# Four heads at a time in the maxima of two blocks, a third pair of PSUM banks, and a new order: a transformer kernel on one core

## The chip, the cores and the metric

The kernel runs on one core of a Trainium2 chip. The metric is the time of one execution on the device, in microseconds (us). The core has five engines, which run their own instruction streams and wait for each other by semaphores: TensorE (PE; PEld is its weight load), VectorE (DVE), ScalarE (ACT), GpSimd (POOL) and SyncE (SP), which here only issues DMAs. Matrix products are written to PSUM, which has eight banks of 128 partitions x 512 numbers of four bytes; VectorE and ScalarE read them from there.

## The reference

Two layers over an input of 4 sequences of 512 tokens with 128 features. Only the first attention is touched by the change; the rest sets the surroundings.

```python
def _L0_attn_ref(x, WQ, WK, WV, WO):                      # 16 heads of 8 features
    Q, K, V = (heads(WQ), heads(WK), heads(WV))
    score = einsum('bhqd,bhkd->bhqk', Q, K) / sqrt(8) + mask      # causal
    score = exp(score - max(score, axis=-1, keepdims=True))
    score = score / sum(score, axis=-1, keepdims=True)
    out = einsum('bhqk,bhkd->bhqd', score, V)
    return out.transpose(0, 2, 1, 3).reshape(B, S, E) @ WO
...
x = x + _L0_attn_ref(_layernorm(x), ...)
x = x + _L0_ffn_ref(_layernorm(x), ...)    # 8 experts, top 2, capacity, gelu, 128 -> 512 -> 128
x = x + _L1_attn_ref(_layernorm(x), ...)   # a gated linear recurrence over time, then a gelu layer
x = x + _L1_ffn_ref(_layernorm(x), ...)    # five ternary matrices, silu and gelu
```

## The kernel before

**Blocks and stages.** The work is cut into four blocks, one for each sequence (`NB` = 4, 512 tokens each, `TB` = 4 tiles of 128). Each block runs through eight stages: `project` (queries, keys, values), `maxima` (the largest score of each row), `weights` (exponentials and the product with the values), `output` (projection, then `route`: which two experts a token goes to, and a scatter of its row to DRAM), `experts` (gather, 8 experts with 176 seats each, gather back), `recurrence` (8 chunks of 128 channels: four products with the tile `rw`, a scan on VectorE), `feed` and `ternary`. The last block's `feed` and `ternary` are done in two halves.

**Who puts the instructions in order.** The stages only record tasks (`Plan.note`). `Plan.order` then walks through time with costs for each operation (`cost`), and takes for the engine that can begin first the task with the largest weight: the longest chain of costs behind it, plus an offset from the table `AHEAD`, one number for each stage and block. What it decides is each engine's fixed order of instructions. It also keeps a model of TensorE's clock and, where TensorE would wait for more than 0.4 us by its costs, puts products of the constant tile `spread` with itself into a free bank (`fillers`; their line is L513). Their results are never read. All recorded instructions are issued by one line, L524, so the profile's groups go by the names of the tiles.

**PSUM.** Pool `p_d` has three single banks (tag `pt`), which nearly every stage uses. Pool `p_s` has two pairs of banks (tag `s`), for the attention: a task that needs a pair takes it from `pair()`. When the attention has ended, the pairs are given to `p_d` as four more banks (`take`). One bank (`po`) collects the product with the values. `Slots` hands the banks out; the planner gives a task that which has been free longest.

**The scores.** Four groups of four heads; a head lies on 32 partitions, so that four products with 32 rows can run side by side in TensorE's array. `maxima` makes for each group and each part of the rows (tile 3; tile 2; tiles 1 and 0) the scores against all keys up to the diagonal, adds the mask by a product with an identity matrix (tile `mask_q`), and reduces with a maximum on VectorE into `mx`. Block 0 does one head at a time in a single bank, so a group has 12 such tasks; the other blocks two heads in a pair. The maxima are split into two rounded parts (`mh`), transposed (`mT`, in block 0 under the tag `hl`), and in `weights` a product with `spread` subtracts them in PSUM. `weights` then works on four heads, with both pairs at once: product, subtraction, one exponential for each pair on ScalarE into `ex`, masking of the diagonal on GpSimd or VectorE, product with the values into `po`.

In the profile's names: `mx<-pt` and `mx<-s` are the reductions, `s<-ks,qs` or `pt<-ks,qs` as an output of TensorE the scores of one of the two stages, `ex<-s` the exponentials, `hT` the experts' Gelu, `xgd<-ya` the scatter, `xg<-xgd` the experts' load, `st<-dec,k` the scans, `r_h_w` and `r_w_w` the ternary weights. ScalarE holds one table of functions at a time; Exp and Gelu are in different ones, and a change is an instruction of its own (ACT_TABLE_LOAD).

Of the kernel before, what the change touches and what calls it, by code (L numbers as in the profile page):

```python
# [20 lines left out]
P = 128  # L21
# [22 lines left out]
def block_kernel(ctx: ExitStack, tc: tile.TileContext, i: dict, out: bass.AP):  # L44
# [9 lines left out]
    class Slots:  # L54


        def __init__(self, pool, tag, count):
            self.pool, self.tag, self.count = pool, tag, count
            self.size, self.dtypes = 0, set()
            self.until = [0.0] * count  # L60
            self.free = list(range(count))
            self.queues = {}

        def lay(self):
            dtype = F32R if F32R in self.dtypes else min(self.dtypes, key=str)
# [1 line left out]
                self.pool.pool.tile([P, self.size], dtype, name=f"{self.tag}_{k}") for k in range(self.count)  # L67
            ]

        def take(self, other):  # L70

            n = other.size // self.size
            self.taken = other, n
            for k in range(other.count):
                for _ in range(n):
                    self.free.append(len(self.until))
                    self.until.append(other.until[k])
            other.free = []

        def lay_taken(self):  # L80
            other, n = self.taken
            for t in other.tiles:
                self.tiles += [t[:, x * self.size : (x + 1) * self.size] for x in range(n)]

    class Lent:


        def __init__(self, slots, shape, dtype):
            self.slots, self.shape, self.dtype = slots, shape, dtype
            self.slot, self.left, self.end = None, 0, 0.0  # L90

        def dims(self, ap):
            if len(self.shape) == 2:
# [104 lines left out]
    class Plan:  # L198
# [142 lines left out]
        def begin(self, task, engine):  # L341

            t = self.now[engine]
            if task.table is not None and task.table != self.table:
                t += TABLE
            for e, r in task.ready.items():
                if e != engine and r > t:
                    t = r
            new = [x for x in task.lents if x.slot is None]
            for lent in new:  # L350
                same = [x for x in new if x.queue is lent.queue]
                free = lent.slots.free
                if len(free) < len(same) or any(x not in same for x in lent.queue[: len(same)]):
                    return None
                t = max(t, sorted(lent.slots.until[k] for k in free)[len(same) - 1])
            return t


# [28 lines left out]
        def order(self):  # L387
# [5 lines left out]
            for task in self.tasks:  # L393
                if task.stage and task.stage[-1].isdigit():
                    task.weight += AHEAD[task.stage[:-1]][int(task.stage[-1])]
            self.now = dict.fromkeys(ENGINES, 0.0)
            self.table, self.dma = None, 0.0
            self.window, self.active, self.warm = 0, 0.0, False
# [13 lines left out]
            while len(self.log) < len(self.tasks):  # L412
# [37 lines left out]
                items, took, after = task.ways[engine]  # L450
                for lent in task.lents:
                    if lent.slot is None:
                        s = lent.slots
                        lent.slot = min(s.free, key=lambda k: s.until[k])
                        s.free.remove(lent.slot)
                        lent.queue.remove(lent)
                if task.table is not None:
                    self.table = task.table
# [19 lines left out]
                for lent in task.lents:  # L478
                    lent.begun = True
                    lent.left -= 1  # L480
                    lent.end = max(lent.end, end)
                    if lent.left == 0:
                        lent.slots.until[lent.slot] = lent.end
                        lent.slots.free.append(lent.slot)
                task.engine = engine
                for e in task.ways:
                    can[e].remove(task)
# [16 lines left out]
        def issue(self):  # L504
            done = self.order()
            for s in self.slots.values():
                s.lay()
            self.slots["p_d", "pt"].lay_taken()
            self.recording = False
            last = None  # L510
            for task in done:
                if isinstance(task, Fill):
                    nc.tensor.matmul(  # L513
                        task.slots.tiles[task.k][:, : task.n], lhsT=spread[:, 0, :],
                        rhs=spread.rearrange("p g n -> p (g n)")[:, : task.n], start=True, stop=True,
                    )
                    continue

                if task.puts and last is not None and last.puts is task.puts:
                    tc.nc.gpsimd.memset(between, 0.0)  # L520
                if task.engine == "POOL":
                    last = task
                for op, args, kw in task.ways[task.engine][0]:
                    task.ins = getattr(getattr(nc, NAMES[task.engine]), op)(  # L524
                        *map(self.real, args), **{k: self.real(v) for k, v in kw.items()}
                    )
                for x in task.puts or ():
                    if x is not task and x.ins is not None:
                        tc.declare_no_dep(task.ins.ins, x.ins.ins, reason="a row of its own for each token and choice")


    AHEAD = {
        "experts": (1093, -30, 183, 214),
        "feed": (-513, -466, 303, -412),
        "maxima": (-14, 173, -113, 124),
        "output": (912, 246, -21, 373),
        "project": (255, -57, 11, -73),
        "recurrence": (69, 208, 89, -280),
        "ternary_0_": (-1, 4, -2, -244),
        "ternary_2_": (0, 0, 0, 147),  # L540
        "weights": (-86, 98, 268, 497),
    }
    TABLE, NEAR, PATIENCE = 1.3, 0.1, 4.0
    NAMES = {"DVE": "vector", "ACT": "scalar", "POOL": "gpsimd", "SP": "sync", "PE": "tensor"}
# [1 line left out]
    def cost(engine, op, out, ins, kw, args):  # L546
# [39 lines left out]
        if op == "tensor_copy":  # L586
            return 0.2 + 8.0e-4 * n, 0.1
        return 0.25 + 2.1e-3 * n if n > 64 else 1.2, 0.1

    plan = Plan()  # L590

# [186 lines left out]
    def maxima(b):  # L778

        mx = At.att.tile([P, TB, NG, NG], F32, tag="mx", name="mx")  # L780
        for g in range(NG):

            n = 1 if b == 0 else 2
            for part in ((3,), (2,), (1, 0)):
                for h in range(NG // n):
                    ps = bank("s1", shape=(P, 1, S)) if b == 0 else pair()
                    at = 0
                    for t in part:
                        product(ps, h, qs[:, g, ts(t, P)], ks[:, g, :], 0, (t + 1) * P, at, start=(at == 0), n=n)
                        at += (t + 1) * P  # L790

                    at, w = part[0] * P, len(part)
                    with one_task():
                        for j in range(n):
                            mm(ps[:, j, at : at + w * P], lhsT=identb, rhs=mask_q[:, : w * P],
                               start=False, stop=True, skip_group_check=True)
                    at = 0
                    for t in part:
                        nc.vector.tensor_reduce(
                            mx[:, t, g, ts(h, n)], ps[:, :, at : at + (t + 1) * P], AX.X, ALU.max, negate=True,  # L800
                        )
                        at += (t + 1) * P
            hi, lo = mh[:, :, :, 2 * g], mh[:, :, :, 2 * g + 1]
            nc.vector.tensor_copy(hi, mx[:, :, g, :])
            nc.vector.tensor_tensor(lo, mx[:, :, g, :], hi, ALU.subtract)
# [756 lines left out]
```

## Time and profile before

| | |
|---|---|
| median of 3 runs | 741.08 us (740.5 to 745.08) |
| the profiled execution | 740.8 us |
| its span, first to last instruction | 739.1 us |
| TensorE busy | 661.6 us (90%), 3698 products in the records |
| VectorE busy | 462.5 us (63%) |
| ScalarE busy | 307.0 us (42%) |
| GpSimd busy | 198.3 us (27%) |
| granted TensorE clock, mean | 0.943 of full speed |
| table loads on ScalarE | 30, 38.5 us |
| filling products (L513) | 95.2 us busy |

A line of a group reads: line, engine, operation, output<-input by the program's names, shapes, count | busy time in us, mean ns of one | idle time of the engine just before them, and what ended it. Busy times are unions of intervals, and matmuls are pipelined, so a busy TensorE is not one at its peak; a product in four-byte numbers is recorded as two. A line of the table of stretches gives for each engine the busy time and, in brackets, the number of instructions, then the granted clock of TensorE (PEclk, 1.00 is full speed), the share of the DMA engines and GB/s.

Where the stages of the first two blocks lie, by the first and last instruction of their tiles: block 0's reductions from 17.6 to 70.4 us, its exponentials from 34.3 to 85.6, its output projection from 91.2; block 1's reductions from 94.7 to 135.7, its exponentials from 141.4 to 202.2, its output projection from 209.8; block 0's experts' Gelu from 132.4 to 192.3. The scans of the four recurrences begin at 227.1, 337.0, 533.2 and 603.1.

### The profile page before, as it was taken

The page shows a single profiled execution, that of the slowest core. Times are in us where ns is not written, and L with a number is a line of the kernel's source. Part 1 is how long each engine was busy: PE and PEld are TensorE (multiplying, and loading weights), DVE is VectorE, ACT ScalarE, POOL GpSimd, SP SyncE. Part 2 cuts the span into 40 slices and gives each one's busy share as a digit, 9 for nine tenths or more (in the row PEclk, how much of TensorE's full clock was granted, in tenths as well). Part 3 has the DMA queues.
Part 4 walks back from the last instruction along what each step waited for, and adds up shares of the span by engine and source line. Part 5 has one row for each costly group of instructions (what it writes and reads, how often), then busy time and mean ns, then how long its engine had stood idle before and what let it go on. Part 6 is the DMA issues. An engine that isn't in the chain of part 4 may idle for free.

```text
span 739.1 us, 10411 instructions
## 1 busy us (share of the span) xinstructions
PE 661.6 (90%) x3698; PEld 407.4 (55%) x3698; DVE 462.5 (63%) x1125; ACT 307.0 (42%) x496; POOL 198.3 (27%) x295
## 2 busy tenths in 40 slices
PE   5999978978887999999999988979899989999795
PEld 2545454644562358553445644777775454557685
DVE  6875498372278775485889771356527776675444
ACT  2134500688631234566351466751552234322222
POOL 3122213183254000163023234127204030113121
PEclk9579995899998999999999999999999999999898
DMA  5630002252311315301200002352343102000000
GB/s 128 180 87 2 1 20 64 86 170 78 93 44 54 92 26 171 115 23 33 61 22 15 1 19 65 104 149 83 86 144 96 44 21 58 8 1 15 1 1 19
DMA packets 72364, 45.78 MB, mean 62 GB/s; under 512 B 9712, under 2 KB 65264, under 8 KB 72304
## 3 DMA queue, kind: packets, MB, share of 16 engines
q1 hardware_dynamic: 69680, 40.58, 19.4%
q0 software_dynamic: 2048, 4.20, 2.0%
q8 instruction: 31, 0.51, 0.3%
q10 hardware_dynamic: 576, 0.26, 0.1%
q14 instruction: 29, 0.24, 0.1%
HBM read 35.45 MB, written 9.57 MB: 61 GB/s over the span
## 4 chain that ended last, share of the span: by engine, by line
PE 40%; DVE 6%; ACT 5%; issue 2%; POOL 1%; DMA 1%; ACTq 0%; DVEq 0%; SPq 0%
PE s L524 18%; PE pt L524 17%; PE s L513 4%; ACT h L524 1%; DVE h L524 1%; PE po L524 1%; POOL xgd L524 1%; ACT L524 1%; DMA xg<-xgd 1%; ACT ex L524 1%; DVE mx L524 1%; DVE hh L524 1%; ACT hT L524 0%; DVE yc L524 0%; DVE f L524 0%
## 5 line engine op out<-in xcount | busy, mean ns | idle before, releaser
L524 PE MATMUL pt<-yTr,rw 128*128 128x512 f32 x192 | 95.8, 616 | 4.4 <-DVE taken L524 3.1
L524 ACT ACTIVATE ex<-s 128x768 f32<-128x768 f32 (+1 forms) x96 | 79.4, 879 | 43.3 <-PE s L524 40.5
L524 DVE TENSOR_REDUCE mx<-s 128x2 f32<-128x512 f32 (+3 forms) x96 | 74.7, 816 | 8.1 <-PE s L524 7.3
L524 POOL TENSOR_SCALAR_AFFINE_SELECT ex<-ex 128x256 f32<-128x256 f32 (+1 forms) x78 | 38.5, 496 | 128.6 <-ACT ex L524 122.5
L524 PEld LDWEIGHTS pt<-yTr,rw 128*128 128x128 f32 x192 | 34.6, 193 | 43.6 <-issue 23.6
L524 POOL DMA_INDIRECT xg<-ygd,rt_at x32 | 33.8, 1057 | 74.5 <-DMA ygd<-xg 66.0
L513 PE MATMUL s<-spread 128*128 128x128 f32 (+1 forms) x214 | 47.2, 360 | 7.4 <-DVE h L524 3.0
L524 POOL TENSOR_TENSOR ln_rs<-ln_rs,mhalf 128x4 f32<-128x4 f32 (+2 forms) x22 | 24.3, 1105 | 107.6 <-DVE ln_rs L524 107.4
L524 PE MATMUL po<-ex,vs 128*9 128x128 f32 (+3 forms) x512 | 50.4, 441 | 0.7 <-DVE ex L524 0.4
L513 PEld LDWEIGHTS s<-spread 128*128 128x128 f32 x214 | 37.4, 203 | 17.6 <-DVE h L524 3.7
L524 PE MATMUL pt<-xT,ew 128*128 128x176 f32 x200 | 41.5, 333 | 5.8 <-ACT hT L524 3.4
L524 ACT ACTIVATE hT<-pt,w_mb 128x176 f32<-128x176 f32 x100 | 34.5, 407 | 25.6 <-PE pt L524 25.0
L524 POOL DMA_INDIRECT xgd<-ya,rt_at x32 | 31.6, 986 | 48.1 <-DVE rt_incl L524 42.0
L524 POOL CAST hh<-h 128x512 fp32r<-128x512 f32 (+1 forms) x19 | 12.0, 638 | 113.2 <-ACT h L524 58.3
L524 ACT ACT_TABLE_LOAD x30 | 38.5, 1283 | 5.2 <-issue 3.1
L524 DVE TENSOR_TENSOR_SCAN st<-dec,k 128x512 f32<-128x512 f32 x32 | 39.3, 1232 | 1.0
L524 PEld LDWEIGHTS pt<-xT,ew 128*128 128x128 f32 x200 | 31.6, 196 | 13.2 <-ACT hT L524 6.8
L524 PE MATMUL s<-ks,qs 32*128 32x256 f32 (+3 forms) x192 | 34.4, 434 | 3.1 <-DVE mx L524 2.4
L524 DVE TENSOR_REDUCE mx<-pt 128x1 f32<-128x256 f32 (+3 forms) x64 | 27.6, 484 | 9.8 <-PE pt L524 9.5
L524 PE MATMUL s<-yTr,rw 128*128 128x512 f32 x64 | 32.0, 606 | 1.2 <-DVE k L524 0.7
L524 PE MATMUL pt<-hT,ew 128*128 128x176 f32 x160 | 30.1, 322 | 3.3 <-ACT hT L524 2.4
L524 PE MATMUL s<-qs,ks 32*128 32x512 f32 (+3 forms) x256 | 27.5, 391 | 3.4 <-ACT ex L524 2.1
(305 smaller groups left out, 1331.2 us busy)
## 6 DMA issues: line engine op xcount, KB each, us to landing
ew<-in_E_dram SPq DMA_DIRECT2D x64, 256.0 KB, 2.9
xg<-xgd SPq DMA_DIRECT2D x4, 704.0 KB, 5.0
ygd<-xg SPq DMA_DIRECT2D x12, 192.0 KB, 2.1
rw<-in_Wk_dram SPq DMA_DIRECT2D x32, 64.0 KB, 2.0
rw<-in_Wv_dram SPq DMA_DIRECT2D x32, 64.0 KB, 1.9
rw<-in_Wq_dram SPq DMA_DIRECT2D x32, 64.0 KB, 1.9
rw<-in_Wg_dram SPq DMA_DIRECT2D x32, 64.0 KB, 2.1
h<-in_h_w_dram SPq DMA_DIRECT2D x8, 256.0 KB, 3.0
```

What stands on the lines that cost most here:

```text
L513: nc.tensor.matmul(task.slots.tiles[task.k][:, : task.n], lhsT=spread[:, 0, :], rhs=spread.rearrange("p g n -> p (g n)")[:, : task.n], sta ...
L524: task.ins = getattr(getattr(nc, NAMES[task.engine]), op)(*map(self.real, args), **{k: self.real(v) for k, v in kw.items()})
```

## The change

Three things are done at once.

1. In blocks 0 and 1 (`FOURS`), `maxima` handles all four heads of a group in one task, in two pairs of banks, with one reduction for each pair and tile. Blocks 2 and 3 stay at two heads.
2. Two of the three single banks of `p_d` are laid out as one tile of 1024 columns (`joint`), so that they can be lent as a third pair to tasks of the stages in `WIDE` (maxima and softmax of blocks 0 and 1) while both are free. `open`, `get` and `put` of `Slots` do the bookkeeping, in the planner's time. Other tasks still use the two banks singly. In the profile the two banks then bear the name `joint` instead of `pt`.
3. The table `AHEAD` has new numbers, so the order of the instructions differs everywhere, in all blocks.

The instructions that do the work are otherwise the same; the line numbers move (L513 to L559, L524 to L570).

```diff
+        def lay_joint(self, lender):
+
+            self.lay()
+            lender.count -= 2
+            lender.lay()
+            lender.count += 2
+            (dtype,) = {t.dtype for t in lender.tiles}
+            both = lender.pool.pool.tile([P, 2 * lender.size], dtype, name="joint")
+            lender.tiles += [both[:, : lender.size], both[:, lender.size :]]
+            self.tiles.append(both)
+
+        def open(self, lent):
+
+            got = [(self.until[k], k) for k in self.free]
+            if self.lender is not None and lent.wide:
+                n = self.lender.count
+                if n - 1 in self.lender.free and n - 2 in self.lender.free:
+                    got.append((max(self.lender.until[n - 2 : n]), self.count))
+            return got
+
+        def get(self, lent, t):
+
+            k = min(self.open(lent), key=lambda x: (max(x[0], t), x[1]))[1]
...
     AHEAD = {
-        "experts": (1093, -30, 183, 214),
-        "feed": (-513, -466, 303, -412),
-        "maxima": (-14, 173, -113, 124),
-        "output": (912, 246, -21, 373),
-        "project": (255, -57, 11, -73),
-        "recurrence": (69, 208, 89, -280),
-        "ternary_0_": (-1, 4, -2, -244),
-        "ternary_2_": (0, 0, 0, 147),
-        "weights": (-86, 98, 268, 497),
+        "experts": (943, 252, 1024, -23),
+        "feed": (-778, 135, -10, -1375),
+        "maxima": (110, 118, -386, 62),
+        "output": (673, 292, 171, 695),
+        "project": (-292, -658, 682, -1001),
+        "recurrence": (260, -843, -240, -730),
+        "ternary_0_": (522, -135, -50, -154),
+        "ternary_2_": (0, 0, 0, 70),
+        "weights": (303, 416, 1206, 155),
     }
...
+    WIDE = {"maxima0", "weights0", "maxima1", "weights1"}
+    FOURS = {0, 1}
...
-            n = 1 if b == 0 else 2
+            n = NG if b in FOURS else 2
             for part in ((3,), (2,), (1, 0)):
                 for h in range(NG // n):
-                    ps = bank("s1", shape=(P, 1, S)) if b == 0 else pair()
+                    pss = [pair() for _ in range(n // 2)]
+                    ps = [p[:, j] for p in pss for j in range(2)]
                     at = 0
                     for t in part:
-                        product(ps, h, qs[:, g, ts(t, P)], ks[:, g, :], 0, (t + 1) * P, at, start=(at == 0), n=n)
+                        with one_task():
+                            for j in range(n):
+                                own = ts(n * h + j, HP)
+                                mm(ps[j][:, at : at + (t + 1) * P], lhsT=qs[own, g, ts(t, P)],
+                                   rhs=ks[own, g, 0 : (t + 1) * P], start=(at == 0), stop=False, skip_group_check=True)
                         at += (t + 1) * P
...
-                    at = 0
-                    for t in part:
-                        nc.vector.tensor_reduce(
-                            mx[:, t, g, ts(h, n)], ps[:, :, at : at + (t + 1) * P], AX.X, ALU.max, negate=True,
-                        )
-                        at += (t + 1) * P
+                    for k, p in enumerate(pss):
+                        at = 0
+                        for t in part:
+                            nc.vector.tensor_reduce(
+                                mx[:, t, g, ts(n // 2 * h + k, 2)], p[:, :, at : at + (t + 1) * P], AX.X, ALU.max,
+                                negate=True,
+                            )
+                            at += (t + 1) * P
```

## The prediction, made before the changed kernel was run

> **What bounds the kernel now.** I read the page's busy rows first, then a table of stretches cut where the stages of block 0 and block 1 begin and end, then the groups of the maxima's reductions and of ScalarE inside those stretches, and last the timeline of TensorE.
>
> The stretches are: maxima and softmax of block 0 (17.6 to 70.8), maxima of block 1 beside block 0's routing (91.2 to 137), experts of block 0 beside the softmax of block 1 (131 to 204), everything up to the last block's recurrence (204 to 599), and the end.
>
> ```profile
> core 0: us, PE busy (x) PEld busy (x) DVE busy (x) ACT busy (x) POOL busy (x), PEclk, DMA share, GB/s
> 17.60:70.80 53.20, 50.52 (x301) 26.26 (x299) 40.12 (x120) 15.64 (x21) 9.78 (x17) 0.74 0.34 98
> 91.20:137.00 45.80, 38.54 (x205) 25.46 (x206) 37.53 (x98) 7.18 (x12) 9.55 (x16) 0.70 0.11 34
> 131.00:204.00 73.00, 61.14 (x473) 39.62 (x472) 28.32 (x62) 53.49 (x77) 30.72 (x45) 0.96 0.37 109
> 204.00:599.00 395.00, 364.90 (x1994) 221.31 (x1994) 258.29 (x628) 175.27 (x295) 112.30 (x148) 0.98 0.24 67
> 599.00:739.10 140.10, 123.36 (x548) 84.33 (x547) 83.07 (x172) 41.10 (x75) 25.08 (x32) 0.96 0.06 16
> ```
>
> Four different limits stand in five rows. In the first, TensorE is busy 50.5 of 53.2 us, much of it at half clock (0.74 granted). In the second VectorE leads (37.5 of 45.8) and TensorE is throttled again. In the third ScalarE carries 53.5 of 73 us. From 204 on TensorE is busy 92% of the time, and it sets the pace.
>
> ```profile
> L524 DVE TENSOR_REDUCE mx<-pt 128x1 f32<-128x512 f32 x16 | 10.3, 686 | 2.8 <-PE pt L524 2.5
> L524 DVE TENSOR_REDUCE mx<-s 128x2 f32<-128x1024 f32 x8 | 9.5, 1219 | 2.5 <-PE s L524 2.5
> L524 DVE TENSOR_REDUCE mx<-pt 128x1 f32<-128x384 f32 x16 | 8.3, 552 | 4.8 <-PE pt L524 4.8
> L524 DVE TENSOR_REDUCE mx<-s 128x2 f32<-128x768 f32 x8 | 7.6, 954 | 0.8 <-PE s L524 0.6
> L524 DVE TENSOR_REDUCE mx<-pt 128x1 f32<-128x256 f32 x16 | 6.0, 417 | 2.2 <-PE pt L524 2.2
> L524 DVE TENSOR_REDUCE mx<-s 128x2 f32<-128x512 f32 x8 | 5.5, 691 | 2.4 <-PE s L524 2.1
> ```
>
> The first form of each size is block 0 (one head), the second block 1 (two heads). Reading two heads at once saves little: 1219 ns against 2 x 686.
>
> ```profile
> L524 ACT ACT_TABLE_LOAD x16 | 20.5, 1283 | 2.2 <-PE pt L524 1.4 <-issue 0.3 <-DVE xg L524 0.2
> L524 ACT ACTIVATE ex<-s 128x768 f32<-128x768 f32 (+1 forms) x24 | 19.9, 879 | 1.7 <-PE s L524 1.5
> L524 ACT ACTIVATE hT<-pt,w_mb 128x176 f32<-128x176 f32 x32 | 11.3, 403 | 10.2 <-PE pt L524 10.1
> ```
>
> These are ScalarE's groups between 131 and 204: switching between Exp and Gelu costs as much (20.5 us) as all 24 exponentials.
>
> **Block 0's maxima.** One head at a time becomes four. TensorE's part shrinks: 64 products of 32 rows took 19.7 us in the first stretch, partly cold; four such products side by side are what the softmax does already (28.9 us for four blocks, 7.2 each). So 12 us leave TensorE; the 48 mask products (9.5 us) stay. VectorE's reductions go from 28.4 us (16 x 0.686, 0.552, 0.417, 0.279) to 26.2 (8 x 1.219, 0.954, 0.691, 0.413).
>
> That stage now hangs on VectorE. A rule speaks against the change here: the Trainium skill, TensorEngine Tiling (Array Packing), Performance Considerations, says that packing speeds TensorE but not the emptying of PSUM, which may become the bottleneck. The rows agree. If TensorE set the pace, the stage would gain 12 us; by the rule it gains 28.4 - 26.2 = 2.2. I take the rule. A set of four heads needs both pairs of banks; in block 0 the lent pair lets the next set be filled while the second half of the last is reduced (TensorE needs some 1.0 us: 0.50 for the products, 0.28 for the first two masks, two hand-overs; a half takes 1.1 to 1.2).
>
> In the order of the changed program the whole of block 0's maxima stands ahead of its first softmax product; before, the two were interleaved. So I add them: 26.2 us of reductions, 1.5 for the four splits, 3.5 for the statistics of blocks 1 and 2 between them, from 17.6: 48.8. Then four groups of softmax at some 10.5 us, from the timeline (three units of products 0.6 to 1.0, two exponentials 1.94 or 1.51, hand-overs 0.4: 3.4 + 2.6 + 2.6; the flip of the output with copy and reciprocal 1.9): 42. The output stage follows at about 94; before, its projection started at 91.2. **Cost 3 us** (bounds: a gain of 5, if groups overlap more; a loss of 12, if each set is 1 us late).
>
> **Block 1's maxima.** The third pair is hardly lent here: in the built order all 24 reductions of block 1 read the two own pairs, and one single exponential of blocks 0 and 1 reads the lent one. A set holds both pairs, so nothing is filled while it is reduced. Per set 1.0 + 2.44, 0.95 + 1.9, 1.25 + 2.2, four times: 39 us, and 8 us of routing on VectorE between them: 47. Before, they took 44 (92.3 to 136.2). **Cost 3 us**, on the start of block 1's softmax. Waiting behind are its first exponentials; the experts of block 0 wait for routing and gather alone, and these keep their place.
>
> **Table loads.** Built, ScalarE has 38 loads before and 28 after; 8 of each belong to the path not taken, so 30 become 20. Of these, 16 become 10 between the start of block 0's experts and the end of block 1's softmax: 6 x 1.283 = 7.7 us less on the engine that carries this stretch. The page on ScalarE: Activation LUTs (What ACT_TABLE_LOAD costs) gives 2.66 us for each switch, with a drain; then it would be 16.0 us. The timeline shows no such drain:
>
> ```profile
> 140.06 1.28 ACT L524 ACT_TABLE_LOAD   x1
> 141.35 1.94 ACT L524 ACTIVATE ex<-s 128x1024 f32<-128x1024 f32 x2
> ```
>
> The next activation starts 1.29 us after the load. I take 7.7. Idle time of ScalarE there is 12 to 20 us, mostly on TensorE; the later start of the softmax (3 us) is hidden in part by the order, which puts 16 Gelus ahead of the first exponential where 8 stood. I count **a gain of 5 us** for the stretch. The other four loads fall after 204, where ScalarE is busy 44%: nothing.
>
> **The rest, from 204.** The work is the same; the order is new. What the order shows is how much TensorE is given to do while it waits: the products of `spread`. Up to block 1's output projection their number rises from 27 of 512 columns and 77 of 128 to 123 and 192: these fill the waits for VectorE of the paragraphs above, so they cost nothing while they fit. After it, it falls from 120 and 124 to 90 and 102. A timeline row prices the wide ones, others the narrow ones (0.15 us, 0.76 for five):
>
> ```profile
> 503.78 9.19 PE L513 MATMUL s<-spread 128*128 128x512 f32 x42 [0.24 <-DVE h L524]
> ```
>
> 0.219 x 30 + 0.15 x 22 = 9.9 us less filling on an engine that is 92% busy. (That very row, 9.2 us long, is a wait with nothing else to do; the new order has no such run after block 1's output.) These are waits that the planner foresaw, not all of those that come, so I take 7 of the 9.9 as **gain** (bounds 0 and 15: the measured idle time there, 30 us, may shrink too).
>
> **Sum**, against the profiled execution (740.8 us, its span 739.1, so 1.7 around it): +3 (block 0), -5 + 3 (experts and softmax of block 1, with its later start), -7 (rest) would be -6; warm clock in block 1's maxima, where a dense filling replaces 27 us at half clock, takes back the 3 us: its products (0.69 to 0.79 us there, 0.44 to 0.50 warm) are on the path of every set, and I had priced them warm but the routing's gaps full. That leaves -9: 740.8 - 9 = **732 us**, 1.2% under the median of 741.08.
>
> **Rivals.**
>
> *No gain that shows.* The waits that the new order avoids come back elsewhere: the end is tied by a chain (last recurrence from 599, feed, two halves of the ternary layer) that loses nothing, and experts of block 3 stand later among TensorE's work than before. ScalarE's saved loads then only lengthen its waits for TensorE (10.1 us before `hT`). For it: from 599 on VectorE is at 59%, no engine is full. Against it: the work left after block 3's experts is also smaller. 740.8 + 3 - 5 = 739.
>
> *More than that.* All 9.9 us of filling, 4 us of the idle time and the full 7.7 us of loads count, and block 0 costs nothing: 740.8 - 21.6 = 719.
>
> *Slower: filling that overruns.* In both maxima stages nearly each of the 24 sets has a run of filling behind it, such as five wide and six narrow products: 5 x 0.219 + 6 x 0.15 = 2.0 us warm, where VectorE gives 1.2 us plus its backlog in block 0, and 2.4 in block 1. If the clock stays at half, as it does in much of these stretches now (0.74, 0.70), it is 3.7 us, and each next set comes 1.3 to 1.9 us late: 24 x 1.6 = 38 us less the 9 of the forecast, some 770; with half of the sets cold about 751. It decides where a run of filling is longer than the reductions that it hides behind, about 2.2 us. For it: the clock; against it: the filling is itself full-array work, which before was nearly absent here (two runs before 68 us).
>
> **Chances.** Forecast 0.45 (own range 727 to 737; two thirds of it under 733.7), no gain 0.23, more 0.15, slower 0.17. A run of this kernel tells about 1% from no change, so: faster 0.45 (0.30 + 0.15), same 0.38 (0.15 + 0.23), slower 0.17. The range takes in most of "more" and the half-cold case: 719 to 752.
>
> **What would show it.** Block 0's output projection at 92 to 96 (over 100: overrun, then reductions `mx` with waits for TensorE over 0.5 us each); granted clock over 0.9 between 17 and 137; 10 table loads in the stretch of block 0's experts, and block 1's output projection at 205 to 209 (now 209.8); TensorE's filling after it about 35 us; the last recurrence starting 5 to 10 us before 599. If the projection of block 1 is early and the end is not, the rest's order is wrong; if it is late, the maxima are.

## The result, and the profile after

| | before | after |
|---|---|---|
| median of 20 runs each, same chip | 743.67 us (740.37 to 747.82) | 747.72 us (742.76 to 752.96) |
| ratio, 95% interval | | **1.0051 [1.0029, 1.0074]** |
| span of the profiled execution | 739.1 us | 742.1 us |
| granted TensorE clock, mean | 0.943 | 0.98 |
| block 0's output projection starts | 91.2 | 91.3 |
| block 1's first exponential | 141.4 | 151.9 |
| block 1's output projection | 209.8 | 215.1 |
| from there to the end | 529.3 | 527.0 |
| table loads on ScalarE | 30 | 20 |

Half a per cent slower, where 1.2% faster was forecast. The stretches of the prediction, in the changed kernel (the last scans now begin at 620, so the cut at 599 is moved to 615):

```profile
core 0: us, PE busy (x) PEld busy (x) DVE busy (x) ACT busy (x) POOL busy (x), PEclk, DMA share, GB/s
17.60:70.80 53.20, 50.67 (x436) 35.60 (x437) 37.03 (x87) 18.83 (x26) 9.65 (x17) 1.00 0.35 97
91.20:137.00 45.80, 41.05 (x254) 31.76 (x254) 32.13 (x90) 7.76 (x15) 9.55 (x16) 0.85 0.13 40
131.00:204.00 73.00, 60.95 (x460) 38.44 (x459) 34.25 (x77) 45.31 (x72) 32.74 (x44) 1.00 0.38 112
204.00:615.00 411.00, 374.44 (x2034) 218.38 (x2033) 262.91 (x640) 176.02 (x299) 114.11 (x146) 0.98 0.23 65
615.00:742.10 127.10, 110.17 (x507) 76.20 (x505) 75.92 (x159) 36.28 (x69) 24.73 (x31) 0.99 0.06 16
```

The clock that had been at 0.74 in block 0's maxima is full, and ScalarE works 45.3 us instead of 53.5 in the third row. The loss is in the fourth, which is 16 us longer (the fifth is 13 shorter, and the cut between them has moved): TensorE has a smaller busy share there (374.4 of 411, 91.1%, against 364.9 of 395, 92.4%), although it has less filling to do (39.1 us behind block 1's output projection, 51.3 before).

The reductions of blocks 0 and 1 together, groups by shape, answer to the six of before:

```profile
L570 DVE TENSOR_REDUCE mx<-s 128x2 f32<-128x1024 f32 x14 | 16.7, 1219 | 8.0 <-PE s L570 5.5 <-PE joint L570 2.5
L570 DVE TENSOR_REDUCE mx<-s 128x2 f32<-128x768 f32 x14 | 12.9, 949 | 2.7 <-PE s L570 2.7
L570 DVE TENSOR_REDUCE mx<-joint 128x2 f32<-128x1024 f32 x2 | 2.4, 1216 | 0.0
```

A reduction costs what it did. Only 8 of the 64 read the lent pair (`joint`), and these wait for nothing. ScalarE between 131 and 204:

```profile
L570 ACT ACT_TABLE_LOAD x10 | 12.8, 1283 | 0.6 <-DVE xg L570 0.5
L570 ACT ACTIVATE hT<-joint,w_mb 128x176 f32<-128x176 f32 x32 | 11.3, 404 | 12.4 <-PE joint L570 12.3
```

Ten loads instead of 16, 1283 ns each as before. And all 32 Gelus now read one tile, `joint`. That name turned out to be the point.

### The profile page after: what moved, and what is told of

It reads as the page before. It is cut to its first block, busy times and chain, and to the rows that moved or that the text cites. A ratio compares the mean times of both kernels' runs of the same rounds, so it can differ in the third digit from the quotient of the medians.

```text
span 742.1 us, 10670 instructions
## 1 busy us (share of the span) xinstructions
PE 658.3 (89%) x3857; PEld 411.1 (55%) x3857; DVE 453.9 (61%) x1095; ACT 296.5 (40%) x490; POOL 201.9 (27%) x292
## 4 chain that ended last, share of the span: by engine, by line
PE 44%; DVE 15%; ACT 7%; issue 4%; POOL 4%; DMA 3%; SPq 0%; ACTq 0%; DVEq 0%; POOLq 0%
PE joint L570 19%; PE pt L570 10%; PE s L570 9%; PE s L559 2%; ACT hT L570 2%; PE po L570 2%; POOL xg L570 2%; DMA xg<-ygd,rt_at 2%; DVE oc L570 2%; DVE k L570 2%; DVE h L570 1%; DVE mx L570 1%; ACT h L570 1%; POOL xgd L570 1%; DVE st L570 1%
## 5 line engine op out<-in xcount | busy, mean ns | idle before, releaser
L570 DVE TENSOR_REDUCE mx<-s 128x2 f32<-128x512 f32 (+3 forms) x120 | 93.1, 816 | 18.6 <-PE s L570 15.8
L570 ACT ACTIVATE ex<-s 128x768 f32<-128x768 f32 (+1 forms) x95 | 78.5, 878 | 46.4 <-PE s L570 37.3
L570 PE MATMUL joint<-yTr,rw 128*128 128x512 f32 x132 | 71.1, 632 | 8.6 <-DVE k L570 5.0
L570 POOL DMA_INDIRECT xg<-ygd,rt_at x32 | 30.9, 966 | 123.0 <-DMA rw<-in_Wv_dram 49.3
L570 POOL TENSOR_SCALAR_AFFINE_SELECT ex<-ex 128x256 f32<-128x256 f32 (+1 forms) x76 | 39.8, 526 | 76.2 <-ACT ex L570 75.6
L570 POOL TENSOR_TENSOR ln_rs<-ln_rs,mhalf 128x4 f32<-128x4 f32 (+2 forms) x22 | 24.5, 1116 | 106.7 <-DVE ln_rs L570 104.0
L570 PE MATMUL po<-ex,vs 128*9 128x128 f32 (+3 forms) x512 | 51.4, 434 | 2.2 <-DVE ex L570 1.2
L570 PE MATMUL pt<-yTr,rw 128*128 128x512 f32 x94 | 51.0, 624 | 0.2
L570 POOL DMA_INDIRECT xgd<-ya,rt_at x32 | 35.3, 1104 | 47.5 <-DVE rt_incl L570 41.6
L559 PE MATMUL s<-spread 128*128 128x128 f32 (+1 forms) x213 | 42.1, 334 | 5.0 <-ACT ex L570 3.3
L570 ACT ACTIVATE hT<-joint,w_mb 128x176 f32<-128x176 f32 x82 | 29.2, 405 | 40.6 <-PE joint L570 35.9
L570 PE MATMUL joint<-xT,ew 128*128 128x176 f32 x164 | 35.0, 330 | 9.5 <-ACT hT L570 6.1
L570 PE MATMUL joint<-hT,ew 128*128 128x176 f32 x184 | 35.9, 325 | 8.3 <-ACT hT L570 7.5
L570 PEld LDWEIGHTS joint<-yTr,rw 128*128 128x128 f32 x132 | 23.1, 195 | 35.8 <-issue 10.5
L559 PE MATMUL joint<-spread 128*128 128x128 f32 (+1 forms) x192 | 39.5, 350 | 2.5 <-DVE taken L570 1.4
L559 PEld LDWEIGHTS s<-spread 128*128 128x128 f32 x213 | 33.5, 191 | 13.4 <-ACT ex L570 4.7
L570 DVE TENSOR_TENSOR_SCAN st<-dec,k 128x512 f32<-128x512 f32 x32 | 39.3, 1230 | 0.8
L559 PEld LDWEIGHTS joint<-spread 128*128 128x128 f32 x192 | 32.0, 199 | 11.2 <-issue 2.9
L570 PEld LDWEIGHTS joint<-hT,ew 128*128 128x128 f32 x184 | 28.1, 189 | 14.3 <-ACT hT L570 12.4
L570 POOL CAST hh<-h 128x512 fp32r<-128x512 f32 (+1 forms) x18 | 11.7, 654 | 86.8 <-ACT h L570 51.9
L570 PEld LDWEIGHTS joint<-xT,ew 128*128 128x128 f32 x164 | 24.9, 189 | 17.6 <-ACT hT L570 11.2
L570 PE MATMUL s<-ks,qs 32*128 32x256 f32 (+3 forms) x240 | 30.6, 401 | 2.4 <-DVE mx L570 2.3
```

Of the source, the lines that this page charges most:

```text
L559: nc.tensor.matmul(task.slots.tiles[task.k][:, : task.n], lhsT=spread[:, 0, :], rhs=spread.rearrange("p g n -> p (g n)")[:, : task.n], sta ...
L570: task.ins = getattr(getattr(nc, NAMES[task.engine]), op)(*map(self.real, args), **{k: self.real(v) for k, v in kw.items()})
```

## The experiments

All ratios are against the kernel before, run on the same chip in the same session; the chips differ by some 2% (before: 743.5 to 756.6 us), so ratios are compared, not times. Where stage times are given, mind the chip: e1 to e4 and e9 to e12 ran on chips on which the kernel before takes 743.5 and 744.9 us, like the result's 743.7; e5 to e8, e13 and e14 on chips on which it takes 756.4 and 756.6, so that their stages look up to 2% too long beside the changed kernel's. e5, e6, e10, e11 and e13 keep the order of the kernel that they change, and e12 and e14 too but for the filling that they drop. In e1 to e4 the planner made a new order; e7, e8 and e9 keep those of e1, e3 and e4.

### Which of the three parts costs

The first theory, from the two traces, was "sets": block 1's sets of four hold both pairs, so VectorE has a gap before each set and block 1's softmax starts 10.5 us late. The rival "table": the new order gives back in the tail what it wins.

**e1_old_table**, the new tasks with the old numbers:

```diff
-        "experts": (943, 252, 1024, -23),
+        "experts": (1093, -30, 183, 214),
...
```

> The changed kernel with the old numbers in AHEAD: four heads at a time in blocks 0 and 1 and the lent pair stay, only the order of the planner goes back where the table decides it (its stretch after block 3's experts then has the same filling as before: 98 wide products and 71 narrow ones). Theory 'sets' (block 1's sets of four heads hold both pairs, nothing is filled while VectorE reduces, so block 1's softmax starts late): first exponential of block 1 at 150 to 154 us (before 141.4, after 151.9), block 1's output projection at 214 to 218, time 746 to 750 us against 743.7 before. Theory 'table' (the new order loses what the new tasks win): first exponential may be late, but the time is 740 to 744. Theory 'noise' (nothing but scatter): ratio to before within 0.998 to 1.002.

Measured: 1.0518 [1.0476, 1.0560]. First exponential of block 1 at 154.7, its output projection at 217.8: front as both theories said. But from there to the end 561.7 us, 32 more than before, where neither theory put a loss; "table", which had said 740 to 744, fell with it.

**e2_old_tasks**, the kernel before with the new numbers:

> The kernel before with the new numbers in AHEAD alone: one head at a time in block 0, two in block 1, nothing lent. Its stretch after block 2 has the same filling as the changed kernel (7 wide products and 9 narrow ones, then 75 and 71). Theory 'sets': the tail's gain stays and nothing is late, so block 1's first exponential at 140 to 146, time 738 to 742, ratio to before 0.993 to 0.999. Theory 'table': time 745 to 750, ratio 1.002 to 1.008. Theory 'noise': within 0.998 to 1.002.

Measured: 1.0016 [0.9993, 1.0038]. Block 0's output projection 107.7, block 1's 237.8 (28 us late), and then 507.4 us to the end: 22 less than before and 20 less than the changed kernel. Yet from block 2's output projection on, TensorE has the very same row of instructions in both (its last 1446 are equal, as are VectorE's last 555 and ScalarE's last 270), and takes 363.7 us here (381.5 to 745.2) and 388.4 there (353.7 to 742.1). The same order, 25 us apart.

**e3_block1_two**, two heads at a time in block 1 only:

```diff
-    FOURS = {0, 1}
+    FOURS = {0}
```

> The changed kernel with two heads at a time in block 1 (FOURS = {0}); block 0's four heads, the lent pair and the new table stay, and so does the filling after block 2. Theory 'sets': block 1's first exponential back to 141 to 146 (after 151.9), block 1's output projection at 206 to 211 (after 215.1), time 740 to 744 against 747.7 after: faster than the changed kernel by 4 to 7 us. Theory 'table': first exponential may be early, the time stays at 746 to 750. Theory 'noise': within 0.2% of the changed kernel.

Measured: 1.0077 [1.0050, 1.0105]. Block 1's first exponential came at 149.3, 2.6 us earlier than with sets of four, but its output projection at 217.6, 2.5 us later, and the time did not drop. "Sets" fell. The time is one that "table" had named (746 to 750), but e1 had already gone against it.

**e4_no_lending**, `WIDE` empty:

> The changed kernel with nothing lent (WIDE empty): block 0's sets too then hold both pairs and wait for VectorE. Theory 'sets': the same gap of about 0.95 us before each set now appears in block 0 as well, its maxima end at 54 to 60 us (after 48.3); since the changed kernel's early end of the maxima brought nothing to block 0's output projection (91.2 before, 91.3 after), the projection comes at 93 to 99 and the time is 748 to 754. If VectorE's pace does not bound block 0 (my prediction's assumption wrong), the projection stays at 91 to 92 and the time at 747 to 748.

Measured: 1.0263 [1.0212, 1.0314]. Block 0's maxima end at 60.8 and its output projection starts at 104.2, 13 us late: in block 0 the third pair carries weight, though only eight reductions read it.

What e1, e3, e4 and the changed kernel share, and e2 and the kernel before do not, is how the banks are laid out: two of the three single banks are one tile, whether lent or not. (They also share block 0's sets of four, but those are over long before the stretch that loses.) In the built program each wait names a point in another engine's row. In the changed kernel, 59 waits of TensorE before a product into one half of `joint` name a reader of the *other* half, and 64 waits of ScalarE and VectorE name another engine's instruction on the other half, 45 of them a product (the expectation of e5 says 71 on a product, which takes in 19 on each other and 7 of ScalarE on itself). No data of the tile pass between them: these are false waits. So a third theory, "joint".

### The joint tile

**e5_single_banks**, order untouched, two tiles of one bank each:

```diff
-            both = lender.pool.pool.tile([P, 2 * lender.size], dtype, name="joint")
-            lender.tiles += [both[:, : lender.size], both[:, lender.size :]]
-            self.tiles.append(both)
+            lender.tiles += [lender.pool.pool.tile([P, lender.size], dtype, name=f"single{k}") for k in range(2)]
+            self.tiles.append(Halves(lender.tiles[-2:]))
...
```

> The changed kernel in its own order on every engine, with the tile joint laid out as two tiles of one bank each. The 8 reductions and the one exponential that read the lent pair are issued as two instructions of one bank each (9 instructions more, about 0.15 us each: 2 x 0.686 against 1.219 for the largest). Theory 'joint' (new: since two banks are one tile, a product into one half waits for the reader of the other half, and a reader for a product in the other half; in the built program 59 waits of TensorE and 71 of ScalarE and VectorE on a product name such an instruction, none here): the stretch from block 1's output projection to the end shrinks from 527 us to 503 to 512 (507.4 in the kernel with the old tasks and the new numbers, which has the same order on TensorE there), time 720 to 733, ratio to before 0.968 to 0.985. Theory 'sets' and theory 'table': nothing changes in what they blame, 746 to 750.

Measured: **0.9479 [0.9439, 0.9518]**. The tail from block 1's output projection: 497.8 us, on one of the slower chips. Both builds put the tiles in the same two banks of PSUM; waits and nine split instructions are all that differs. "Joint" held, and the gain was larger than it said.

**e6_before_joint**, the kernel before with only this layout:

```diff
+            s = self.slots["p_d", "pt"]
+            s.count -= 2
...
+            both = s.pool.pool.tile([P, 2 * s.size], s.tiles[0].dtype, name="joint")
+            s.tiles[1:1] = [both[:, : s.size], both[:, s.size :]]
```

> The kernel before in its own order, with two of its three single banks laid out as one tile of 1024 columns, as in the changed kernel; nothing is lent and no task is changed. Theory 'joint': 137 waits of TensorE then name a reader of the other half, more than twice as many as in the changed kernel, since block 0's maxima go through these banks too: 765 to 790 us, ratio 1.03 to 1.06, with VectorE's and ScalarE's waits for TensorE up in all stages. If one tile costs nothing by itself (the 20 us of the tail come from elsewhere, such as which bank a task got): 742 to 745.

Measured: **1.1761 [1.1704, 1.1819]**, some three times the most that was expected (1.06). TensorE's waits for `hT` in the kernel before, then the largest in e6 (total us, times, longest):

```profile
PE pt L524 <- ACT hT L524: 5.8, 10, 1.1
```

```profile
PE joint L528 <- ACT hT L528: 16.3, 31, 1.1
PE joint L528 <- ACT g L528: 8.8, 9, 1.6
...
PE joint L528 <- DVE mx L528: 5.7, 11, 1.0
```

The granted clock fell to 0.868, where the runs of the kernel before on that chip have 0.93 on average. That may be part of why the size was missed; it was not taken apart.

**e7_old_table_single**, e1 with single banks:

> New tasks and lending with the old numbers in AHEAD (781.6 us with the joint tile), with the joint tile laid out as two single banks, order untouched. Theory 'joint': the tail from block 1's output projection, 561.7 us with the joint tile, returns to the 529.3 of the kernel before or less; time 738 to 750. If it stays above 770, the old table's order itself does not go with the new tasks and the joint tile is not the cause of the 38 us.

Measured: 1.0014 [0.9982, 1.0046], 756.9 us: against e1's 1.0518 the joint tile was its whole loss (the expected times meant a chip on which the kernel before takes 743; on this one it took 756.4). New tasks and lending alone bring nothing, new numbers alone (e2) bring nothing, both together 5.2% (e5).

**e8_block1_two_single**, e3 with single banks:

> Block 1 with two heads at a time (748.8 us with the joint tile), with the joint tile laid out as two single banks, order untouched. Beside e5 this tells what block 1's sets of four are worth when the joint tile is out of the way. Theory 'sets': faster than e5 by 3 to 7 us. If sets of four are right for block 1 too: slower than e5 by 0 to 5 us (with the joint tile its output projection came at 217.6 against 215.1). Theory 'joint' for its own time: 722 to 735.

Measured: 0.9563 [0.9523, 0.9604], on the same chip as e5: 723.1 against 717.0 us. With this table, four heads at a time in block 1 are worth 0.9%; they do not cost. The order is not the same in the two: e8 has 26 table loads and e5 20, so the 0.9% is not the sets' alone. The late first exponential, which I had taken for the cause, is made up before block 1's output projection (e3 against the changed kernel).

**e9_no_lending_single**, e4 with single banks:

> The changed kernel with nothing lent (760.8 us with the joint tile) and all three banks single. With the joint tile, going without the lent pair cost 13 us, nearly all of it before block 0's output projection (104.2 against 91.3). If lending is worth that by itself, the ratio to before is 0.96 to 0.97 (e5's 0.948 and 13 us); if the joint tile was part of those 13 us, it is 0.945 to 0.955, as e5, and then four heads and the new numbers need no third pair at all.

Measured: 0.9768 [0.9728, 0.9808]: without the joint tile lending is worth 3%, more than expected (the planner's order differs too). Block 0's output projection came at 105.0.

**e13_joint_while_lent**, the joint tile given up after its last use as a pair, no instruction added:

```diff
+            self.joint.close()
+            pool = work.enter_context(tc.tile_pool(name="p_k", bufs=1, space=PSUM))
+            lender.tiles[lender.count - 2 : lender.count] = [
+                pool.tile([P, lender.size], lender.tiles[0].dtype, name=f"single{k}") for k in range(2)
+            ]
```

> The changed kernel in its own order on every engine, with the joint tile kept until the last task that reads it as a pair (an exponential of block 0) and two single banks laid out in its place from there on. No instruction is added. If the joint tile costs nothing while it is lent and all of its price lies in the stages after, as the stage times say (block 0's and block 1's output projections at 91.3 and 215.1 with it, at 93.3 and 218.0 without it in e5): ratio to before 0.942 to 0.952, block 0's output projection within 2 us of e5's 93.3. If the waits that it makes in block 0's stages, or the split instructions of e5, decide: above 0.96, or under 0.94.

Measured: 0.9494 [0.9459, 0.9530]. This is the clean pair: the same instructions in the same order on every engine as in the changed kernel. (The tiles lie in other banks than there; in e5 they do not, and it gains the same.) Against 1.0051 that is 5.6% of the time of the kernel before, some 41 us. The two profiles, 742.1 and 713.0 us, show only 29 of it, since e13 ran on a slower chip (before: 756.6).

Where the price lies, the output projections tell: at 91.1, 216.0 and 353.7 (changed kernel 91.3, 215.1, 353.7), then block 3's at 495.4 instead of 511.3, the end at 713.0 instead of 742.1. The slower chip hides some of it. e10 below has the same order without the joint tile and ran on a chip like the changed kernel's (744.9): its four stretches from block 0's output projection on take 120.9, 137.7, 142.3 and 209.0 us against 123.8, 138.6, 157.6 and 230.8. So some 4 us lie ahead of block 2's output projection and 37 behind it. The two stretches behind block 2's output projection, first the changed kernel, then e13 (columns as in the table above):

```profile
353.70:511.30 157.60, 141.72 (x810) 79.47 (x811) 99.81 (x231) 73.84 (x120) 41.58 (x54) 0.99 0.22 61
511.30:742.10 230.80, 203.71 (x902) 137.73 (x900) 132.83 (x312) 70.35 (x139) 55.50 (x66) 1.00 0.14 40
```

```profile
353.70:495.40 141.70, 134.70 (x811) 79.14 (x810) 99.20 (x232) 74.14 (x120) 41.28 (x54) 1.00 0.24 68
495.40:713.00 217.60, 200.31 (x902) 140.34 (x900) 132.93 (x312) 70.59 (x139) 54.37 (x66) 0.97 0.15 43
```

The counts are the same but for single records and the busy times of VectorE and ScalarE nearly so, and it is 29 us less, on the slower chip. TensorE's waits (total us, times, longest) in the changed kernel:

```profile
PE joint L570 <- ACT hT L570: 14.1, 29, 1.1
...
PE joint L570 <- DVE k L570: 7.8, 7, 2.3
PE joint L570 <- DVE oc L570: 3.7, 6, 1.4
```

and in e13:

```profile
PE single L587 <- ACT hT L587: 6.3, 11, 1.1
PE single L587 <- DVE k L587: 3.3, 1, 3.3
...
PE single L587 <- DVE oc L587: 1.2, 2, 0.7
```

How such a wait looks on TensorE's timeline (start, duration, what ran, in brackets the idle time before and its releaser), in block 2's experts of the changed kernel:

```profile
428.40 0.76 PE L570 MATMUL pt<-hT,ew 128*128 128x176 f32 x4
429.66 0.57 PE L570 MATMUL joint<-xT,ew 128*128 128x176 f32 x2 [0.50 <-ACT hT L570]
430.72 0.86 PE L570 MATMUL joint<-xT,ew 128*128 128x176 f32 x4 [0.50 <-ACT hT L570]
432.14 0.57 PE L570 MATMUL joint<-xT,ew 128*128 128x176 f32 x2 [0.56 <-ACT hT L570]
432.55 0.46 PE L570 MATMUL pt<-hT,ew 128*128 128x176 f32 x2
```

and the same products in e13:

```profile
420.78 0.76 PE L587 MATMUL pt<-hT,ew 128*128 128x176 f32 x4
421.44 1.46 PE L587 MATMUL single<-xT,ew 128*128 128x176 f32 x8
422.74 0.46 PE L587 MATMUL pt<-hT,ew 128*128 128x176 f32 x2
```

The products `xT,ew` do not read `hT`. They go into one half of `joint` while a Gelu reads an earlier result from the other, so TensorE and ScalarE take turns, with 0.50 to 0.56 us of idle TensorE at each. In e13 the eight run through. From the first line to the last it takes 1.96 us there and 4.15 in the changed kernel: three false waits cost 2.2 us, 0.7 each, more than the idle time that the rows show.

### Where else halves wait for each other, and what filling costs

The kernel before does the same with the two pairs: after the attention they are used as four single banks, still halves of two tiles. **e11_before_freed** lays four tiles of one bank in their place at that moment:

```diff
-            for t in other.tiles:
-                self.tiles += [t[:, x * self.size : (x + 1) * self.size] for x in range(n)]
+            other.pool.stack.close()
+            pool = work.enter_context(tc.tile_pool(name="p_t", bufs=1, space=PSUM))
+            self.tiles[self.count :] = [
+                pool.tile([P, self.size], self.tiles[0].dtype, name=f"t_{k}") for k in range(n * other.count)
+            ]
```

> The same for the kernel before: its order, with the two pairs laid out anew as four single banks after the attention. Here 77 waits of TensorE and some 40 of ScalarE and VectorE name an instruction of the other half. At some 0.2 us each: 15 to 25 us less, ratio 0.967 to 0.980; as a rival, nothing (0.998 to 1.002), if these waits end before another that the same instruction has anyway.

Measured: **0.9672 [0.9636, 0.9708]**. The kernel before gains 3.3% with the order of its computing engines as it was; from block 3's output projection to the end it takes 238.3 us instead of 261.9.

**e10_five_freed**, the same edit on e5:

> e5 in its own order on every engine; when the attention has ended and its two pairs become four single banks, their tiles are given back and four tiles of one bank are laid out in their place (before, they stayed halves of two tiles). In e5 25 waits of TensorE and some 26 of ScalarE and VectorE still name an instruction of the other half there. If they cost what those of the joint tile cost (29 us of the tail for 59 and 71, some 0.2 us each): 5 to 12 us less than e5, ratio to before 0.932 to 0.942. If with seven banks a product seldom takes a bank whose neighbour is still being read: as e5, 0.944 to 0.952.

Measured: 0.9490 [0.9451, 0.9530], as a ratio no different from e5, which ran on another chip. In e5 25 such waits of TensorE were left where the kernel before has 77; why they cost nothing in this order was not taken apart.

e10 and e11 are a pair that tells more. They ran on one chip in one session, and no wait on another half is left in either, so what lies between them is the new tasks with the lending, and the new table: 704.8 against 719.7 us, 2.1%. The front is equal (block 1's output projection at 213.9 and 214.2); the gain is in the stretch behind it, first e11, then e10:

```profile
214.20:719.10 504.90, 475.90 (x2518) 306.20 (x2514) 338.41 (x791) 213.40 (x367) 132.78 (x174) 0.97 0.20 57
213.90:702.90 489.00, 458.87 (x2456) 290.33 (x2454) 329.97 (x769) 205.84 (x360) 134.62 (x172) 0.98 0.20 58
```

It is 15.9 us shorter, with 17.0 us less busy time of TensorE, of which 9.5 is filling (48.4 and 38.9 us).

**e12_before_no_tail_fill**, the kernel before without filling products behind block 1's softmax:

```diff
+            last = max(k for k, stage in enumerate(stages) if stage == "weights1")
+            done = [task for k, task in enumerate(done) if k < last or not isinstance(task, Fill)]
```

> The kernel before in its own order without the 120 wide and 124 narrow filling products that stand after the last task of block 1's softmax (no result depends on them). It tests the term of my sum that gave 7 us for 30 wide and 22 narrow ones less: by that term, 120 x 0.219 + 124 x 0.15 = 44.9 us of filling, 7 in 9.9 of it on the path, 30 us less, ratio 0.955 to 0.965. If filling stands only where TensorE waits anyway, nothing on the path, 0.995 to 1.002; if its warmth counts (granted clock falls under 0.9 in the tail), 1.005 to 1.04.

Measured: 0.9923 [0.9902, 0.9943], between the expectations: 5.7 us for 44.9 us of filling. The stretch from 209.8 (208.2 here) had 484.3 us of busy TensorE at a clock of 0.97; now

```profile
208.20:735.10 526.90, 461.02 (x2274) 276.02 (x2270) 338.19 (x791) 214.47 (x367) 132.73 (x174) 0.94 0.19 54
```

it has 23.3 us less busy time, at 0.94. Of the 51.3 us in which TensorE was busy with filling, 10.5 had overlapped with products of the work; 17.5 went into longer products (the work alone is busy for 461.0 us instead of 443.5), 20.9 into idle time, and 2.4 were won in this stretch.

**e14_five_no_tail_fill**, the same on e10:

> e10 (single banks, pairs laid out anew after the attention, own order) without the 90 wide and 102 narrow filling products after the last task of block 1's softmax. In the kernel before, dropping 45 us of filling there brought 0.8%, some 6 us, 13% of it. At that share 90 x 0.219 + 102 x 0.15 = 35 us of filling are worth 4 to 5 us: ratio 0.938 to 0.946. If the new order's TensorE is tighter, as my prediction had it (7 in 9.9): 25 us, 0.910 to 0.920. If the filling is needed for the clock: above 0.950, with a granted clock under 0.93 in the tail.

Measured: 0.9444 [0.9417, 0.9472]. Beside e10's 0.9490 some 3 us, not told apart with certainty (the intervals meet); the 25 us are excluded. By its ratio it is the fastest kernel here, with e5, e10 and e13 close behind.

## Why the prediction was wrong, point by point

- **Block 0, +3 predicted, 0 measured.** The maxima ended at 48.3 us; I had 48.8. The softmax behind took 36.2 us from first to last exponential where I had put 42 for its groups in all; the projection came at 91.3, not 94. The rule that VectorE, not TensorE, sets this stage held: once the reductions have begun at 19.6, VectorE waits for TensorE only once, for 0.26 us. It held because of the third pair: without it the projection is 12 to 13 us later (e4, e9). A slip had no effect: 16 x (0.686 + 0.552 + 0.417 + 0.279) is 30.9 us, not 28.4, which is the busy time; the gain "by the rule" would have been 4.7, and it did not enter the sum.
- **Block 1's maxima, +3 - 3 predicted.** The stage took 46.8 us, as worked out (47), but before it had taken 41.0 between the first and last reduction, not the 44 that I set against it; it began 3.1 us later; and the clock reached 0.85, so the warmth that was to take 3 us back came in part. (The reductions of that block are 32, not 24.) The first exponential was 10.5 us late. It was not what made the kernel slower: without the joint tile, sets of four here go with a gain of 0.9% (e8). The sign that I had set for this term, a late output projection of block 1, came (215.1) and pointed to the wrong place.
- **Table loads, -5 predicted, -5.8 measured**: the exponentials of block 1 span 55.0 us instead of 60.8, with six loads of 1283 ns fewer. The size was right; the cause was shown only in part, for 8 Gelus also moved ahead of the first exponential (16 instead of 24 lie in that span, 0.35 us each, 2.8 us), and no run takes the loads alone away.
- **The rest, -7 predicted, -2.3 measured: the step that failed.** It began "The work is the same; the order is new." The work was the same; its waits were not. The joint tile stood in the diff, I had written that other tasks still use its two banks singly, and the sum has it at nothing, without a reason. It cost 38 us of this stretch: 527.0 us with it, 489.0 in the same order without it (e10, on a like chip; freeing the pairs too brought nothing beside e5). The kernel before had false waits too, in the two pairs, and they were not in the sum either: 529.3 us with them, 504.9 without (e11), so 24.4. What the sum did price, the new order and its tasks, brought 15.9 (504.9 to 489.0), over twice the 7 and just over the bound of 15. Together: -24.4 - 15.9 + 38.0 = -2.3.
- **Could it have been priced?** In size, yes. The waits of the built order name what each product waits for, and 59 of TensorE's named a reader of a bank that the product does not touch. At the 0.58 us of a wait for `hT` in the profile of before (5.8 us in 10) that is 34 us, several times the gain forecast for the stretch; 38 was measured. The rate is no bound, and was taken afterwards: for the 137 of e6 it gives 79 us, and 131 was measured.
- **The filling.** 9.9 us less was expected from the counts, and 9.5 less was measured (e11 to e10), with idle time equal (29.0 and 30.1 us). As a sign of waits that the order no longer has, it pointed the right way. Taken as a load on TensorE it would have misled: where filling alone is dropped and the waits stay (e12), 13% of it comes back as time.
- **The rivals.** "No gain that shows" ended nearest (739 against a profiled 743.8), and it did say that the avoided waits come back; but the waits that came were the joint tile's, which it did not name. "More than that" (719) lay nearer to what order and tasks reach without the joint tile, 706 (0.9494 of 743.7). Filling that overruns did not happen: block 0's reductions hardly wait and the clock there is full. That "no gain" came so near is luck: the gain of the order and two sets of false waits, which none of the rivals had, happen to cancel.

So the change is three things: new tasks and a new table, which together bring 5.1% (e13; 2.1% where the kernel before is rid of its own false waits), and a layout that costs 5.6% (1.0051 against 0.9494).

## What to carry to other kernels

Two buffers that become one tile share their readers and writers, so an order made for separate buffers can then make engines take turns: before costing a change of layout, read the waits of the built order, and look for one whose target touches neither the operands nor the bank. A buffer that has to be joined for one stage can be given up when the stage ends (e13), and the same is worth looking for in what was there before (e11: 3.3%). Two kernels with the same order in a stretch and different times (here e2 and the changed kernel) are a pair worth having: neither order nor work can be the cause.

## What the runs showed of the hardware that was not expected

One false wait shows as 0.50 to 0.56 us of idle TensorE in the timeline and costs 0.7 there; the 137 of TensorE in e6, with those of the reading engines, cost 131 us in all (887.3 against 756.4), near 1 us for each of the 137, together with a granted clock of 0.868 instead of 0.93. And the filling in the tail of the kernel before, 51 us of busy TensorE, is worth little either way: without it the clock there falls from 0.97 to 0.94 (0.98 to 0.95 in the new order) and the time still drops by 0.8% (0.5%, not certain).
